# Two graph layers in fp32: ones multiplied ahead of the work, one pool per pair of x's operands, PSUM read first at the ends of phases, and row blocks spread within a step

## The chip, the core and the metric

The kernel runs on one core of one Trainium2 chip. The metric is the device time of one execution in microseconds (us), of which the median of several runs is given. Lower is better. PE is the matrix engine (TensorE), PEld its weight loads, DVE the VectorE, ACT the ScalarE, POOL the GpSimd engine and SP the SyncE, which only issues transfers here. A name with a q (SPq) is that engine's sequencer.

## The reference

x is 4096 x 512, adj is 4096 x 4096, sparse in its values but treated as dense, W is 512 x 512. All are fp32. Unused parts are left out.

```python
def _layernorm(x, axis=-1, eps=1e-5): ...

def layer0(cur, incidence_m):
    head = (incidence_m > 0).astype(incidence_m.dtype)
    head = head / jnp.maximum(jnp.sqrt(jnp.sum(head * head, axis=-1, keepdims=True)), EPS)
    inc = incidence_m + head
    return (inc @ cur) / jnp.sum(inc, axis=-1, keepdims=True)

def layer1(X, A, W):
    A2 = A + jnp.eye(A.shape[0], dtype=A.dtype)
    dscale = jnp.diagonal(A2) ** (-0.5)
    temp = A2 @ X @ W.T
    A_norm = dscale[:, None] * A2 * dscale[None, :]
    return jax.nn.relu(A_norm @ temp)

x = _layernorm(x + layer0(x, adj), axis=-1)
x = _layernorm(x + layer1(x, adj, W), axis=-1)
```

So there are three large products: inc times x, A2 times the first layer's result, and A_norm times the projected result.

## The kernel before

**Fewer products.** The big products are done by a Strassen-like scheme (the Winograd form): a 2 x 2 block product takes seven block products, with sums of the left operand (S1 to S4, made by `add_up`, L163) and of the right operand (T1 to T4). Each of the seven has a PSUM bank of its own (`bank(0)` to `bank(6)`); `bank(7)`, also called `spare()`, serves counts, projections and transposes.

**Layer 0 (n up to 63, L450 and L437).** x's operands lie in eight tiles `feats`, one for two row blocks each, all from one pool `feats_pool` (L273). `build` and `build_last` make the T sums in them. The adjacency comes in chunks of four times 128 x 512 by SP. For row block 0 (`multiply_plain`, L439) there is no scheme: it runs 2 halves x 4 chunks x 4 row steps with plain products. The positive entries of its rows are counted by `count_half` (L318): ACT makes signs, PE multiplies them by a bf16 tile of ones, `scale_half` makes the scale from the counts, and `upper_inc` or `to_inc` adds the scaled mask. For the later blocks the counts come from rows loaded as they lie (`load_natural`, a prefetch of five tiles); `count` sums signs on ACT, and `spread` (L355) makes the scale in three parts: reduce and square root, reciprocal and a diagonal tile `d`, and a product of `d` with the fp32 ones (L373). `raw_sums` also writes sums of the adjacency out to memory for layer 1, by POOL. From block 1 on `multiply1` (L423) does seven products for each of 16 row steps, and `combine` (L461) reads the seven banks.

**Layer 1 (L823 to L881).** Both products of layer 1 (k=2 and k=3) use the scheme twice, nested: 7 outer products (`p`, in the order of `ORDER`), for two column slabs `s`, each with 8 steps `kk`. In a step `multiply2` (L250) does the seven inner products of 512 columns. Its left tiles come from `tr` (loaded by `load_b`, L235) and `ts` (made from it by `sum_b`), its right tiles from `a` (loaded by `load`) and `s` (made by `prepare`, two steps ahead). After the last step of a phase `outer` (L660) takes the banks: `inner` (L639) has four outputs, made by four of its operations, which a function `put` receives; for k=2 the results of p=6 go straight to c12 and three more operations follow for each of the four (`then`, L682).

**The order around the change.** The program is in manual order: each engine executes its instructions as the Python code issues them, and pools take the place of pools that were closed. At the end of layer 0 `scope.close()` (L623) frees the operands of x, and `tops` (the pool of `tr` and `ts`), `ringx`, `workx`, `accs` and `resident` are opened in their place. In each step of layer 1 the order is: loads on SP, `prepare`, `sum_b`, what `later` holds, `multiply2`, and then one finished row block from `queue`, or two in the last phase:

```python
        while later:
            later.pop(0)()
        multiply2(n, acc)
        ...
        end = n >= len(steps) - NQ
        if 1 <= kk <= (6 if end else 5):
            for _ in range(2 if end else 1):
                if queue:
                    kind, args = queue.pop(0)
                    fetch(kind, *args)
                    kind(*args)
```

A row block is a projection (`project`, k=2) or a row block of the output (`layer1`, or `layer1_first` for half columns of two blocks). The latter transposes on PE (L746) into the spare bank, and ACT rectifies from there (L750). What remains of it (`rest`: the sum, statistics, square root, normalisation, the store; for a projection the sums and their write) is held in `later` and runs in the next step. After the last step `finish` (L797) completes the last eight row blocks.

Of the kernel before, what the change touches and what calls it, by code (L numbers as in the profile page):

```python
# [8 lines left out]
F32 = mybir.dt.float32  # L9
# [4 lines left out]
P = 128  # L14
# [12 lines left out]
def tile_adj_resnorm_d2(  # L27
# [67 lines left out]
    def spare():  # L95
        return bank(7)
# [150 lines left out]
        nc.vector.tensor_add(t[:, :, 3, :], b[:, :, 2, :], t[:, :, 2, :])  # L247
        sums_b[g] = t

    def multiply2(n, acc):  # L250
        k, s, p, kk = steps[n]
        a, sm = ready.pop(n)
        b, t = (y[n // 2][:, kk % 2] for y in (raw_b, sums_b))
        for m, (right, left) in enumerate((
            (a[:, A11, :], b[:, 0, :]), (a[:, A12, :], b[:, 2, :]), (sm[:, S2, :], t[:, 2, :]),
            (sm[:, S1, :], t[:, 0, :]), (sm[:, S3, :], t[:, 1, :]), (sm[:, S4, :], b[:, 3, :]),
            (a[:, A22, :], t[:, 3, :]),
        )):
            nc.tensor.matmul(acc[m], left, right, start=(kk == 0), stop=(kk == NQ - 1))  # L259

    def load_up_to(n):
# [4 lines left out]
    def load_b_up_to(g):  # L266
        while made["load_b"] <= min(g, len(groups) - 1):
            load_b(made["load_b"])
            made["load_b"] += 1


    scope = ExitStack()
    feats_pool = scope.enter_context(tc.tile_pool(name="feats", bufs=1))  # L273
    w1_pool = scope.enter_context(tc.tile_pool(name="w1", bufs=2))
    pools["turn"], pools["work"] = [ring] * 2, work

# [21 lines left out]
    def build(g):  # L298

        s = feats[g][:, :, :, 0:H]  # L300
        nc.vector.tensor_sub(s[:, :, T1:T3 + 1:2, :], s[:, :, B11:B22 + 1:2, :],
                             s[:, :, T4:T4 + 1, :].to_broadcast([P, 2, 2, H]))
        nc.vector.scalar_tensor_tensor(s[:, :, T2, :], s[:, :, T1, :], -1.0, s[:, :, B22, :], op0=ALU.mult, op1=ALU.subtract)

    def build_last(g):

        s = feats[g][:, :, :, 0:H]
        nc.vector.tensor_add(s[:, :, T4, :], s[:, :, B21, :], s[:, :, T2, :])
# [9 lines left out]
    def count_half(h, c, ps):  # L318

        m = w1_pool.tile([P, 2, CW], F32, name="sr", bufs=2).bitcast(BF16)[:, :, 0:CW]  # L320
        signs(m, chunks[c][:, 2 * h:2 * h + 2, :])
        for z in range(2):
            nc.tensor.matmul(ps, ones_b, m[:, z, :], start=(c + z == 0), stop=(c == NC - 1 and z == 1))

    def scale_half(h, ps):
        n = scale[0][:, h, :]
# [75 lines left out]
    def to_inc(n, h):  # L402

        y, z = masks(n, h, slice(0, CW))
        nc.vector.tensor_add(z, z, y)  # L405
# [30 lines left out]
            )):  # L436
                nc.tensor.matmul(acc[m][:, 0:w], left, b[:, right, 0:w], start=(kk == 0), stop=(kk == NP - 1))  # L437

    def multiply_plain(h, c, acc, then=None):  # L439

        a = chunks[c]
        for i in range(CK):
            kk = c * CK + i
            cols = slice(i * P, (i + 1) * P)
            if then is not None and i == 1:
                then()
            k1, k2 = (a[:, A21, cols], a[:, A22, cols]) if h else (inc11[:, c, cols], a[:, A12, cols])
            for left, ops in ((k1, (B11, T4)), (k2, (B21, B22))):
                for y, op, w in zip(acc, ops, (W, H)):
                    nc.tensor.matmul(y[:, 0:w], left, slots[kk][:, op, 0:w], start=(kk == 0 and left is k1),  # L450
                                     stop=(kk == NP - 1 and left is k2))
# [55 lines left out]
        nc.gpsimd.dma_start(out=in_outer(2, j, slice(T1, T4 + 1)), in_=t)  # L507


    feats = [feats_pool.tile([P, 2, 7, W], F32, name=f"b{g}") for g in range(NP // 2)]  # L510
    for kk in range(NP):
        slots[kk] = feats[kk // 2][:, kk % 2]
    for n in range(NC):
# [9 lines left out]
    for c in range(NC):  # L523
        load_half(0, c)
    ps = spare()
    for c in range(NC):
        count_half(0, c, ps)
    for kk in range(10):
        load_x(kk)
    for c in range(NC):  # L530
# [18 lines left out]
    build(2)  # L549
    upper_inc(3, slice(0, CW))  # L550
    ps = spare()
    multiply_plain(0, 2, top, lambda: [count_half(1, c, ps) for c in range(NC)])
    build(3)
    scale_half(1, ps)
    count(16)
    build(4)
    raw_sums(0)
    to_inc(0, 1)
    multiply_plain(0, 3, top)
    top = take(0, top)  # L560
    build(5)
# [1 line left out]
    to_inc(1, 1)  # L563
    multiply_plain(1, 0, low)
    load_chunk(NC)
    spread(1, 0)
    build(6)
    build_last(0)
    raw_sums(2)
    to_inc(2, 1)  # L570
    spread(1, 1)
    build_last(1)
    multiply_plain(1, 1, low)
    load_chunk(NC + 1)
    spread(1, 2)
# [84 lines left out]
    def outer(k, p, acc):  # L660

        (c11, c12), (c21, c22) = C_of[k]

        def into(dst, then=None):
            def put(i, op):
                op(dst[:, i, :])
                if then is not None:
                    then(i)
            inner(acc, put)

        def by_way(then):
            def put(i, op):
                y = row_tile("y", 2)
                op(y)
                then(i, y)
            inner(acc, put)

        if k == 2:
            if p in (4, 5, 1):
                into({4: c21, 5: c22, 1: c11}[p])  # L680
            elif p == 6:
                def then(i):  # L682
                    add(c12[:, i, :], c11[:, i, :])
                    nc.vector.tensor_sub(c21[:, i, :], c21[:, i, :], c12[:, i, :])
                    add(c12[:, i, :], c22[:, i, :])
                into(c12, then)
            elif p == 7:
                def then(i, y):
                    nc.vector.tensor_sub(c21[:, i, :], c21[:, i, :], y)
                    less(c22[:, i, :], y, c12[:, i, :])  # L690
                by_way(then)
            else:
                dst = {2: c11, 3: c12}[p]
                by_way(lambda i, y: add(dst[:, i, :], y))
        else:
            if p in (2, 3):
                into({2: c11, 3: c12}[p])
            elif p == 5:
                into(c22, lambda i: add(c12[:, i, :], c22[:, i, :]))
            elif p == 1:  # L700
                into(c21, lambda i: add(c11[:, i, :], c21[:, i, :]))
            elif p == 6:
                def then(i, y):
                    add(c21[:, i, :], y)
                    add(c12[:, i, :], c21[:, i, :])
                by_way(then)
            elif p == 7:
                def then(i, y):
                    add(c21[:, i, :], y)
                    less(c22[:, i, :], c22[:, i, :], c21[:, i, :])  # L710
                by_way(then)
            else:
                by_way(lambda i, y: nc.vector.tensor_sub(c21[:, i, :], y, c21[:, i, :]))
# [83 lines left out]
    def finish(h, items):  # L797

        stats = {}
        for t in range(len(items) + 2):  # L800
# [16 lines left out]
            if t > 1:  # L817
# [2 lines left out]
                normalise(o, *stats[b])  # L820
                nc.sync.dma_start(out=out[b * P:(b + 1) * P, :], in_=o)

    load_b_up_to(0)  # L823
    load_up_to(2)
    load_b_up_to(2)
# [4 lines left out]
    for n, (k, s, p, kk) in enumerate(steps):  # L830
        if kk == 0:
            acc = [bank(m) for m in range(7)]
        load_up_to(n + LA + PF)
        if n + LA < len(steps):
            prepare(n + LA)
        if n % 2 == 0 and n // 2 + 1 < len(groups):
            sum_b(n // 2 + 1)
        while later:
            later.pop(0)()
        multiply2(n, acc)  # L840
        if n == 0:
            layer0(NP - 1, C)
        elif n == 1:
            operands(NP - 1, C)
            nc.gpsimd.dma_start(out=wt, in_=w_t.rearrange("(a p) o -> p a o", p=P))
        if n % 2 == 1:
            load_b_up_to(n // 2 + 3)
        end = n >= len(steps) - NQ
        if 1 <= kk <= (6 if end else 5):
            for _ in range(2 if end else 1):  # L850
                if queue:
                    kind, args = queue.pop(0)
                    fetch(kind, *args)
                    kind(*args)
            for kind, args in queue[:2]:
                fetch(kind, *args)
        if kk == NQ - 1:
            outer(k, p, acc)
            if (k, p) in DONE:
                h = DONE[k, p]  # L860
                items = blocks(h, s)
                if n + 1 < len(steps):
                    queue.extend(((project, layer1)[k - 2], (h, b)) for b in items)
            if n == len(steps) - 1 - NQ:
                items = sorted(blocks(1, s), key=lambda b: b[1])
                queue.extend((layer1_first, (1, *items[i:i + 2])) for i in range(0, len(items), 2))
            for kind, args in queue[:2]:
                fetch(kind, *args)
        if n + 1 == len(steps) // 2:

            scope.close()
            ring3 = ctx.enter_context(tc.tile_pool(name="ring3", bufs=2))
            late["pool"] = ctx.enter_context(tc.tile_pool(name="late", bufs=1))
            i = made["a"] % 4
            pools["turn"] = [ring3] * 2 + pools["turn"][i:] + pools["turn"][:i]
            made["a"] = 0
            PF = 3
    while later:
        later.pop(0)()
    assert not queue  # L880
    finish(1, items)  # L881


# [30 lines left out]
```

## Time and profile before

| | us |
|---|---|
| median of 3 runs | 2327.46 (2325.59 to 2328.12) |
| the profiled execution, own time | 2326.3 |
| its span in the profile | 2324.4 |
| PE busy | 2278.8 (98%) |
| PE weight loads busy | 1355.4 (58%) |
| DVE busy | 1817.9 (78%) |
| ACT busy | 353.7 (15%) |
| POOL busy | 220.3 (9%) |
| chain that ended last | PE 93%, DVE 4%, DMA 2%, issue 1% |

All times in the views are counted from the start of the span. A row of a timeline has the start, the length, the engine, the line of the code, the operation, output and inputs by the program's names, their sizes and the count; in brackets stands the idle time of the engine before it, and what ended that. In the chain of waits a row has the start, the length, the engine (or DMA) and the line. An fp32 product of the code is two matmul instructions on PE. The granted clock is the share of the full PE clock.

### The profile page before, as it was taken

To read this page: it belongs to the slowest core of one execution; us is meant where nothing else is said; L and a number is where in the kernel's file an instruction comes from. 1 tells how busy PE (TensorE), PEld (TensorE's weight loads), DVE (VectorE), ACT (ScalarE), POOL (GpSimd) and SP (SyncE) were. 2 spreads that over 40 slices of the span, in tenths; PEclk is the share of its full clock that TensorE was granted. 3 is DMA by queue.
4 is the path that set the end of the run, shared out by engine and by line. 5 is a ranking of instruction groups with operands and counts; after the bars stand their busy time and mean duration, and the time that the engine had idled before them with its cause. 6 is when DMAs were issued, how large, how long until landed. Compare 5 with 4: busy or idle time off the path is not lost.

```text
span 2324.4 us, 21026 instructions
## 1 busy us (share of the span) xinstructions
PE 2278.8 (98%) x7182; PEld 1355.4 (58%) x7182; DVE 1817.9 (78%) x2631; ACT 353.7 (15%) x815; POOL 220.3 (9%) x357
## 2 busy tenths in 40 slices
PE   7999999999999999999999999999999999999996
PEld 6888888888888834444444444444444444444443
DVE  5998988989988777787666778776567798767796
ACT  4323322333222000000000000000000011200013
POOL 0111111111111100000111000011100000000010
PEclk9999999999999999999999999999999999999998
DMA  9777777777776466575566746477665576765572
GB/s 319 253 263 252 251 265 257 243 255 265 262 247 223 167 261 263 199 261 201 205 254 252 275 180 253 160 276 266 231 236 215 219 256 241 262 238 212 219 262 77
DMA packets 148443, 551.93 MB, mean 237 GB/s; under 512 B 15968, under 2 KB 24176, under 8 KB 109936
## 3 DMA queue, kind: packets, MB, share of 16 engines
q1 hardware_dynamic: 114624, 417.38, 51.2%
q0 software_dynamic: 33712, 133.21, 15.6%
q8 instruction: 57, 0.93, 0.2%
q14 instruction: 50, 0.41, 0.0%
HBM read 437.27 MB, written 113.25 MB: 237 GB/s over the span
## 4 chain that ended last, share of the span: by engine, by line
PE 93%; DVE 4%; DMA 2%; issue 1%; ACT 0%; SPq 0%; ACTq 0%; DVEq 0%
PE q L259 54%; PE q L437 31%; PE q L726 5%; PE q L450 2%; DMA a<-oa 1%; DVE s L166 1%; PE q L746 1%; DMA a<-adj_r 0%; DVE c L654 0%; DMA s<-adj_q 0%; DVE s L168 0%; PE q L373 0%; DMA a<-adj_q 0%; DVE c L658 0%; DVE r L232 0%
## 5 line engine op out<-in xcount | busy, mean ns | idle before, releaser
L259 PE MATMUL q<-s,ts 128*128 128x512 f32 x1344 | 614.5, 593 | 2.0 <-DVE u L645 1.9
L437 PE MATMUL q<-b,s 128*128 128x256 f32 (+1 forms) x1920 | 454.4, 379 | 0.2 <-DVE s L168 0.2
L166 DVE TENSOR_TENSOR s<-a 128x1024 f32<-128x1024 f32 x236 | 288.8, 1224 | 207.5 <-PE q L259 169.5
L259 PEld LDWEIGHTS q<-s,ts 128*128 128x128 f32 x1344 | 256.0, 191 | 325.5 <-issue 295.7
L437 PEld LDWEIGHTS q<-b,s 128*128 128x128 f32 x1920 | 363.8, 190 | 52.6 <-DVE s L168 0.6
L437 PE MATMUL q<-b,a 128*128 128x258 f32 (+1 forms) x1440 | 354.0, 380 | 0.0
L259 PE MATMUL q<-a,tr 128*128 128x512 f32 x704 | 334.8, 598 | 5.3 <-DMA tr<-ob 4.3
L437 PEld LDWEIGHTS q<-b,a 128*128 128x128 f32 x1440 | 273.3, 190 | 38.5
L259 PE MATMUL q<-s,tr 128*128 128x512 f32 x448 | 228.9, 593 | 0.0
L259 PEld LDWEIGHTS q<-a,tr 128*128 128x128 f32 x704 | 132.8, 192 | 163.4 <-issue 157.8
L312 ACT ACTIVATE nat<-nat,tiny 128x512 f32<-128x512 f32 x240 | 171.0, 715 | 181.4 <-DMA nat<-adj 180.6
L259 PE MATMUL q<-a,ts 128*128 128x512 f32 x352 | 180.3, 594 | 3.3 <-DVE c L650 2.9
L168 DVE TENSOR_TENSOR s<-a,s 128x512 f32<-128x512 f32 x236 | 163.3, 692 | 8.1
L169 DVE TENSOR_TENSOR s<-a,s 128x512 f32<-128x512 f32 x236 | 163.3, 692 | 8.0
L398 DVE SCALAR_TENSOR_TENSOR mask<-a,sc 128x1024 f32<-128x1024 f32 (+2 forms) x129 | 154.2, 1197 | 2.1
L405 DVE TENSOR_TENSOR a<-a,mask 128x1024 f32<-128x1024 f32 x123 | 150.7, 1225 | 6.6 <-DVE mask L398 0.5
L259 PEld LDWEIGHTS q<-s,tr 128*128 128x128 f32 x448 | 85.3, 190 | 107.0 <-issue 100.8
L643 ACT COPY p<-q 128x512 f32<-128x512 f32 x28 | 16.4, 585 | 756.0 <-PE q L259 756.0
L259 PEld LDWEIGHTS q<-a,ts 128*128 128x128 f32 x352 | 66.7, 190 | 88.7 <-issue 76.4
L726 PE MATMUL q<-wt,c 128*128 128x512 f32 x256 | 115.1, 593 | 0.0
L166 DVE TENSOR_TENSOR s<-r 128x1024 f32<-128x1024 f32 x48 | 58.7, 1224 | 68.7 <-PE q L259 62.4
L388 POOL DMA_DIRECT2D oa<-sr x64 | 57.7, 901 | 390.2 <-DVE sr L381 250.8
(134 smaller groups left out, 1695.0 us busy)
## 6 DMA issues: line engine op xcount, KB each, us to landing
a<-adj_r SPq DMA_DIRECT2D x112, 1024.0 KB, 6.1
a<-oa SPq DMA_DIRECT2D x80, 1024.0 KB, 5.3
nat<-adj SPq DMA_DIRECT2D x240, 256.0 KB, 7.2
a<-adj_q SPq DMA_DIRECT2D x60, 1024.0 KB, 6.0
tr<-ob SPq DMA_DIRECT2D x112, 512.0 KB, 3.7
oa<-sr POOLq DMA_DIRECT2D x64, 512.0 KB, 7.9
oa<-r POOLq DMA_DIRECT2D x32, 1024.0 KB, 6.7
y<-x POOLq DMA_DIRECT2D x64, 256.0 KB, 7.2
```

The costliest lines, as they stand in the source:

```text
L166: nc.vector.tensor_add(s[:, S3:S1 + 1, :], a[:, A11:A22 + 1, :], a[:, A21, :].unsqueeze(1).to_broadcast([P, 2, w]))
L168: nc.vector.tensor_add(s[:, S2, :], a[:, A11, :], s[:, S1, :])
L169: nc.vector.tensor_add(s[:, S4, :], a[:, A12, :], s[:, S2, :])
L259: nc.tensor.matmul(acc[m], left, right, start=(kk == 0), stop=(kk == NQ - 1))
L312: nc.scalar.activation(y, a, AF.Sign, bias=tiny, scale=2.0 ** 64, accum_out=accum)
L388: nc.gpsimd.dma_start(out=dst, in_=sr.rearrange("p m (k i) -> p (m k) i", i=P))
L398: nc.vector.scalar_tensor_tensor(m, v, 0.0, s.unsqueeze(1).to_broadcast(list(v.shape)), op0=ALU.is_gt, op1=ALU.mult)
L405: nc.vector.tensor_add(z, z, y)
L437: nc.tensor.matmul(acc[m][:, 0:w], left, b[:, right, 0:w], start=(kk == 0), stop=(kk == NP - 1))
L450: nc.tensor.matmul(y[:, 0:w], left, slots[kk][:, op, 0:w], start=(kk == 0 and left is k1), stop=(kk == NP - 1 and left is k2))
L726: nc.tensor.matmul(pv, C_of[2][h][f][:, 2 * r + e, cols], wt[:, 2 * f + e, :], start=(f + e == 0), stop=(f + e == 2))
L746: nc.tensor.transpose(ps[:, at + i * P:at + (i + 1) * P], C_of[3][h][d // 2][:, 2 * r + d % 2, cols], ident)
```

## The change

It has five parts.

1. `idle_products` multiplies the fp32 tile of ones by itself into a bank that is not in use: 8 times before the first counts, 3 times after each of the first three counts and 11 times after the fourth.
2. Each of the eight tiles of x's operands has a pool of its own.
3. In `multiply_plain(0, 2, ...)` the second counts are taken two by two, ahead of row steps 0 and 2, not all four ahead of step 1. `build(4)` goes behind `to_inc(0, 1)`; `spread(1, 0)` goes behind `to_inc(2, 1)`, and `build_last(1)` ahead of `spread(1, 1)`.
4. `into` lets `inner` make all four outputs before it runs `then` for the four.
5. In each step of layer 1 the row blocks are taken out of the queue ahead of `multiply2`. Of two, the first is done inside `multiply2`, ahead of its fourth product, the second after it. The rests of the step before run after the new row blocks, not ahead of `multiply2`.

```diff
-    def multiply2(n, acc):
+    def multiply2(n, acc, between=None):
...
+            if m == 3 and between is not None:
+                between()
             nc.tensor.matmul(acc[m], left, right, start=(kk == 0), stop=(kk == NQ - 1))
...
-    feats_pool = scope.enter_context(tc.tile_pool(name="feats", bufs=1))
+    feats_pools = [scope.enter_context(tc.tile_pool(name=f"feats{g}", bufs=1)) for g in range(NP // 2)]
...
+    def idle_products(times):
+        for _ in range(times):
+            nc.tensor.matmul(bank(2)[:, 0:P], ones_f, ones_f, start=True, stop=True)
...
-    def multiply_plain(h, c, acc, then=None):
+    def multiply_plain(h, c, acc, then={}):
...
-            if then is not None and i == 1:
-                then()
+            if i in then:
+                then[i]()
...
-    feats = [feats_pool.tile([P, 2, 7, W], F32, name=f"b{g}") for g in range(NP // 2)]
+    feats = [pool.tile([P, 2, 7, W], F32, name=f"b{g}") for g, pool in enumerate(feats_pools)]
...
     ps = spare()
+    idle_products(8)
     for c in range(NC):
         count_half(0, c, ps)
+        idle_products(3 if c < NC - 1 else 11)
...
-    multiply_plain(0, 2, top, lambda: [count_half(1, c, ps) for c in range(NC)])
+    multiply_plain(0, 2, top, {i: lambda i=i: [count_half(1, c, ps) for c in (i, i + 1)] for i in (0, 2)})
     build(3)
     scale_half(1, ps)
     count(16)
-    build(4)
     raw_sums(0)
     to_inc(0, 1)
+    build(4)
...
     load_chunk(NC)
-    spread(1, 0)
     build(6)
     build_last(0)
     raw_sums(2)
     to_inc(2, 1)
+    spread(1, 0)
+    build_last(1)
     spread(1, 1)
-    build_last(1)
     multiply_plain(1, 1, low)
...
         def into(dst, then=None):
-            def put(i, op):
-                op(dst[:, i, :])
-                if then is not None:
+            inner(acc, lambda i, op: op(dst[:, i, :]))
+            if then is not None:
+                for i in range(4):
                     then(i)
-            inner(acc, put)
...
+    def take_up(item):
+        kind, args = item
+        fetch(kind, *args)
+        kind(*args)
...
-        while later:
-            later.pop(0)()
-        multiply2(n, acc)
+        end = n >= len(steps) - NQ
+        items = [queue.pop(0) for _ in range(min(len(queue), 2 if end else 1))] if 1 <= kk <= (6 if end else 5) else []
+        held = later[:]
+        later.clear()
+        multiply2(n, acc, (lambda: take_up(items.pop(0))) if len(items) > 1 else None)
...
-        end = n >= len(steps) - NQ
+        for item in items:
+            take_up(item)
+        for rest in held:
+            rest()
         if 1 <= kk <= (6 if end else 5):
-            for _ in range(2 if end else 1):
-                if queue:
-                    kind, args = queue.pop(0)
-                    fetch(kind, *args)
-                    kind(*args)
             for kind, args in queue[:2]:
                 fetch(kind, *args)
...
-    finish(1, items)
+    finish(1, blocks(1, s))
```

The list that `finish` gets is the same one, under another name.

## The prediction

> **What bounds the kernel now.** I read the profile from the coarse to the fine. First the stretches by stage, since a mean over the span hides where an engine stops. Columns: stretch, length, busy time (and instructions) of PE, PEld, DVE, ACT, POOL, granted clock, DMA share, GB/s.
>
> ```profile
> core 0: us, PE busy (x) PEld busy (x) DVE busy (x) ACT busy (x) POOL busy (x), PEclk, DMA share, GB/s
> 0.00:80.00 80.00, 65.64 (x277) 53.13 (x278) 54.05 (x69) 28.26 (x60) 8.01 (x35) 1.00 0.95 317
> 80.00:813.00 733.00, 732.82 (x3384) 641.32 (x3383) 647.20 (x919) 211.78 (x561) 116.97 (x164) 1.00 0.73 245
> 813.00:860.00 47.00, 41.60 (x92) 17.79 (x91) 31.04 (x58) 2.21 (x5) 3.87 (x6) 0.93 0.70 267
> 860.00:2255.00 1395.00, 1389.84 (x3298) 619.20 (x3297) 1037.68 (x1476) 90.83 (x149) 86.61 (x143) 1.00 0.64 235
> 2255.00:2305.00 50.00, 44.77 (x121) 21.05 (x120) 33.99 (x66) 9.79 (x19) 4.81 (x9) 0.97 0.26 95
> 2305.00:2324.40 19.40, 4.15 (x17) 2.92 (x15) 13.90 (x47) 10.84 (x24) 0.00 (x0) 0.59 0.29 108
> ```
>
> PE is the bound: 2123 of 2128 us in the two long stretches. The change leaves their products alone, so it can only win in the 80 us in front, the 47 at the layer change, the 50 at the end, and 5.2 us of holes between. What makes each hole is in the chain that ended last (start, length, what):
>
> ```profile
> 750.30 63.70 PE q L437 x294
> 814.06 4.07 DMA tr<-ob
> 818.26 2.04 PE q L259 x2
> ...
> 1012.04 1.24 DVE s L166
> ...
> 1021.25 0.70 DVE c L684
> 1023.32 30.35 PE q L259 x70
> ```
>
> At 814.06 the last product of layer 0 ends and only then is `tr` loaded. At 1012 to 1023 the chain lies on DVE. Then the timelines: PE in front and at the end (start, length, count, idle before and releaser), and DVE at two places.
>
> ```profile
> 17.56 1.92 PE L450 MATMUL q<-b,a 128*128 128x258 f32 x4
> 22.95 1.03 PE L450 MATMUL q<-b,a 128*128 128x258 f32 x4
> ```
>
> ```profile
> 2266.44 0.60 PE L746 MATMUL q<-ident,c 128*128 128x128 f32 x4
> 2270.52 0.89 PE L746 MATMUL q<-ident,c 128*128 128x128 f32 x4 [3.48 <-ACT o L750]
> 2271.20 3.38 PE L259 MATMUL q<-a,tr 128*128 128x512 f32 x4
> ```
>
> ```profile
> 57.93 0.17 DVE L359 TENSOR_REDUCE n<-cnt 128x2 f32<-128x16 f32 x1 [6.54 <-ACT nat L312]
> ```
>
> ```profile
> 1014.64 0.68 DVE L644 TENSOR_TENSOR c<-q,p 128x512 f32<-128x512 f32 x1
> ...
> 1031.45 0.42 DVE L246 SCALAR_TENSOR_TENSOR ts<-ts,tr 128x256 f32<-128x256 f32 x1
> ```
>
> L450 starts one instruction per 0.43 us until 21.4, and per 0.216 after: half clock at first. (The clock column shows 1.00 there only because no record precedes 21.4.) The same after the two long idles: 818.3 to 823.5 and 2270.8 to 2274.2 have clock 0.50.
>
> **Front (ones, counts, spread).** An fp32 product is two PE instructions. No row has a 128-column fp32 product, so I bound it: below by the 128-column transposes (0.212 us per instruction at half clock, 0.109 at full), above by the 256-column L450 (0.43, 0.216). I take the transposes, since L450 to L259 show time going with columns. Eight products then take 3.4 us from 2.6, when `ones_f` is set, and end at 6.0, before the first counts (6.39); three between counts take 1.3 us slow, 0.65 fast. With PE some 90% busy from 2.6 on, I put the clock up at about 8. The last count still waits for its signs (11.23) and ends near 11.7 instead of 12.29, so the first L450 moves from 15.71 to 15.1; eleven products (2.4 us) fill most of that wait.
> From there PE needs 16 row steps at 8 x 0.216 = 1.73: 27.7 us, plus 1.7 for the second counts. Those lost 3.35 us at 34.2 to 37.6, as the third signs waited for the first count's buffer (two `sr`). Now ACT has two steps, 3.5 us, for its 2.3 us of signs, whose data landed by about 30. So layer 0's first half ends at 44.5 instead of 49.7: 5.2 earlier (0.6 start, 2.8 clock, 1.7 counts). The DVE keeps up: `to_inc(0,1)` ends near 40.8 and `to_inc(1,1)` near 48.2, for use at 44.5 and 51.5.
> What is late next: `spread(1,0)` needs 16 row counts, paced by their loads, until 57.9. Before, DVE stood there 6.5 us with `build(6)`, `build_last(0)`, `raw_sums(2)`, `to_inc(2,1)` (6.0 us) queued behind it; now they come first. `d` is then ready at 59.75 instead of 64.9, while PE arrives at 58.4: PE waits 1.35 us (before 1.4). DVE's work from 57.9 to the first S2 of block 1 shrinks from 22.8 to about 17 us, S2 at about 75.2 instead of 80.7. Front gain 5.4. Against it: three `raw_sums` writes now fall into the counting instead of two. DMA share there is 0.93 to 0.96. The Trainium skill (DMA: Bandwidth & Descriptors, Issuing engines are not separate DMA queues) says that transfers of all issuers share the same 16 engines and interleave; by it 0.5 MB at 310 GB/s costs up to 1.7 us, by the trace's five-deep prefetch perhaps nothing. I take 0.8: **front 4.6** (2 to 6.5).
> A second rule: TensorE: Matmul & The Clock Gate, Part 1, asks about 3.4 us of sustained work in a free-running window for full clock. The trace has dense work from 15.71 and full clock only at 21.42. If the broken pattern of ones is not enough, PE is 2.8 us later at the spread, of which 1.35 was waiting: 1.5 lost. By the rule alone 0.
>
> **Pools apart.** One pool held all of x's operands, so `tr` waited for the last reader at 814.06. The eight pools are 14.4 KB per partition each; `tr`, `ts` and the extra `a` lie over the first two, last read in the block's first chunk, before 778. SP reaches `tr` right after the load at 801.9; nothing on SP stands in front. DVE is idle from 804.2, so `sum_b(0)` is done early and `combine` follows PE's last products, ending at about 815 instead of 822.7. PE goes on at 814.0: the second step starts at 820.0 instead of 827.16, **7.1** (4.3 wait, 2.8 half clock, which goes since there is no idle). Late next: step 5's `a`, behind `tr` of group 3 on SP, which waits for the POOL writes of the last rows. Before: PE lost 1.4 at 850.8. That chain moves with `combine`, 20.3 us after its end, so `tr` issues at 835.3 and PE needs step 5 at 844.1, 0.6 us more room than before; fewer transfers are bunched behind it. I take **0.5** (-0.3 to 1.4).
>
> **PSUM first.** Only `into` with a `then` changes, and only k=2, p=6 had holes: 3.0 us at 1016 to 1023, 2.5 at 1411 to 1418. With seven reads in 4.9 us PE does not wait in the next step. But the twelve other operations (8.3 us) still run before the next `prepare` and `sum_b`. DVE has no gap from 1012.04 to 1031.9, and in the next phase's third step PE took the S2 product at 1032.01, 0.1 us after `ts` was ready (1031.45 and 0.42). So the wait goes to that product, two steps on. All that remains is the tighter order on DVE (0.61 instead of 0.72 us between independent operations), about 0.4 each: **0.8** (0 to 5.5).
>
> **Row blocks spaced.** In the last phase two blocks per step shared one PSUM bank back to back; rectify (0.69) lay between, and at 2266.9 it also queued on ACT behind the square roots and normalisations of the step before. Now one comes after three products (2.57 us), one after the other four (3.43), and the held rests come behind both rectifies on ACT. From 2252.50: step 2 at 2259.38 (was 2260.43), step 3 at 2266.27 (2271.20), step 4 at 2273.15 (2280.74), step 5 at 2279.6 (2287.18). Closest is the second transpose of step 3 at 2272.7, whose bank is free at 2271.9. `prepare` for step 5 ends near 2273.3: no DVE bound. **7.6** (4 to 8): 5.4 waits, 1.5 half clock, 0.7 small. Of the tail from 2305 nothing changes.
> Holding the rests also moves them elsewhere. On POOL, a projection's write of `t` is queued behind the next block's writes: it lands about 5.6 us into the next step, where DVE wants `t` at 2.6 to 4.1; done by 7.9 of a 9.44 us step. In layer 1, the square root waits on ACT for the next rectify, so DVE stands until 7.5 us into the step and starts the next `prepare` about 1.4 late; `prepare` is two steps (12.9 us) ahead of its use. Both at nothing; without that cover 1.4 per step.
>
> **Sum.** 4.6 + 7.1 + 0.5 + 0.8 + 7.6 = 20.6. The profiled execution took 2326.3 (span 2324.4): 2305.7. The median of the runs lies 1.2 above it: 2306.9, say 2307.
>
> **Rivals.** (1) The pools do not come free apart: `tr` still at 814.06. For it: nothing but that the trace has no case of split pools; against: `tr` waited for the last reader of all, as one pool would. Loses 7.6: 2314.5. (2) The PSUM order wins its full 5.5, if DVE finds slack I do not see: 2302. Against: the gapless DVE run. (3) The front gives 1 to 2 only, its counts later by their DMAs or the clock still half: 2310. (4) Slower: the held square roots. Place: about 20 single blocks of layer 1; DVE stands 1.4 us in each. Should that lateness reach PE, 20 x 1.4 = 28 us is lost and the time is 2335. It decides once DVE is over 11 us late at a `prepare`; I find 1.4, not growing, because a late DVE waits less.
>
> **How the numbers follow.** A measurement of this kernel can tell about 0.2%, 4.7 us. The sum as worked out 0.68, within 4 us; (1) 0.09; (2) 0.07; (3) 0.09; (4) 0.05; nothing gained in all 0.02. Faster 0.93, same 0.02, slower 0.05. The range 2300 to 2312.5 takes in the first, (2) and (3).
>
> **What would show it.** L450 at 0.216 us from its first instruction; no wait of ACT signs for PE near 35; the spread still waiting about 1.3 us, for DVE. `tr` issued near 802 less the front's gain, clock 1.00 throughout the layer change. At p=6 no hole in the next phase's first step, but one of about 2.6 us at its third step's S2, waiting for `ts`. No wait for ACT at L746 before the tail. The prediction is wrong if `tr` still waits for L437, if PE stops in single-block steps, or if the holes at p=6 go without a later one.

## Result and profile after

The changed kernel takes 2314.41 us (median of 11 runs, 2311.66 to 2323.46); the kernel before took 2328.12 in its 11 runs beside it (2325.59 to 2330.42). The ratio is 0.9952, 95% interval 0.9939 to 0.9965: faster, by 13.7 us where 20.5 were forecast, and 1.9 us above the range that was given (2300 to 2312.5). The profiled execution took 2313.43 us, its span is 2311.4, 13.0 shorter than before.

First the same stretches by stage, of the kernel after (length, busy time and instructions of PE, PEld, DVE, ACT and POOL, granted clock, DMA share, GB/s). The fifth stretch is cut at 2295, as its end moved.

```profile
0.00:80.00 80.00, 75.99 (x320) 60.95 (x322) 53.92 (x68) 27.29 (x57) 8.01 (x35) 1.00 0.91 306
...
813.00:860.00 47.00, 46.48 (x116) 21.48 (x115) 36.07 (x66) 2.80 (x6) 3.87 (x6) 1.00 0.77 291
860.00:2255.00 1395.00, 1389.71 (x3304) 618.42 (x3303) 1030.78 (x1474) 90.64 (x151) 86.56 (x143) 1.00 0.64 234
2255.00:2295.00 40.00, 37.85 (x105) 17.48 (x103) 33.35 (x65) 8.90 (x18) 4.81 (x9) 1.00 0.26 93
```

In the layer change PE now has 46.48 of 47 us busy, at clock 1.00, where it had 41.60 at 0.93; the end is at 1.00 too. The first row misleads: PE has 10 us more busy time in the front, and none of it is work that the result needs. The long stretch still lacks 5.3 us of PE, as it did before.

The chain that ended last, after (start, length, what), at the four places where it was shown of before, and at the front:

```profile
8.59 0.80 PE q L331 x2
...
24.18 0.49 PE q L331 x2
24.67 5.42 PE q L458 x25
...
752.48 63.68 PE q L445 x294
816.16 21.99 PE q L261 x52
838.15 8.46 DMA a<-adj_r
...
1024.91 21.74 PE q L261 x50
```

At 816.16 the chain goes from PE to PE: the transfer of `tr` is gone from it. The transfer at 838.15 is that of step 5's `a`, which stood in the chain before as well. But layer 0's last product ends at 816.16 instead of 814.06, so the front has lost 2.1 us instead of gaining 4.6. The front's chain says why: it is made of L331, the products on ones, that were to lie in PE's idle time. The timeline of PE in front, first two rows of before, then after (start, length, count, in brackets idle time before and releaser):

```profile
6.39 1.01 PE L323 MATMUL q<-sr,ones_b 128*128 128x512 bf16 x2 [6.39 <-ACT sr L312]
...
15.71 2.05 PE L450 MATMUL q<-b,s 128*128 128x258 f32 x4 [3.43 <-issue]
```

```profile
2.61 6.77 PE L331 MATMUL q<-ones_f 128*128 128x128 f32 x16 [2.61 <-POOL b L545]
9.17 1.06 PE L326 MATMUL q<-sr,ones_b 128*128 128x512 bf16 x2
10.03 2.34 PE L331 MATMUL q<-ones_f 128*128 128x128 f32 x6
12.16 1.06 PE L326 MATMUL q<-sr,ones_b 128*128 128x512 bf16 x2
...
18.13 0.85 PE L326 MATMUL q<-sr,ones_b 128*128 128x512 bf16 x2
18.82 5.85 PE L331 MATMUL q<-ones_f 128*128 128x128 f32 x22
24.50 1.03 PE L458 MATMUL q<-b,s 128*128 128x258 f32 x4
```

PE's row after shows no idle time, and yet sixteen instructions take 6.77 us. One product (two instructions) follows another after 0.85 us at half clock, and after 0.55 at full. The counts (L326) start at 9.17, 12.16, 15.15 and 18.13; before, they started at 6.39, 7.59, 10.00 and 11.27. The first row product (L458) starts at 24.50, before at 15.71. Lengths tell the clock: six L331 take 2.34 us up to 18.3, and 22 take 5.85 after; the record of the granted clock goes to full at 18.63. What hides in the gapless PE row is in the row of the weight loads:

```profile
2.61 0.50 PEld L331 LDWEIGHTS q<-ones_f 128*128 128x128 f32 x2 [2.61 <-POOL b L545]
3.46 0.50 PEld L331 LDWEIGHTS q<-ones_f 128*128 128x128 f32 x2 [0.35 <-PE q L331]
```

Each product waits 0.35 us with its weights for the product before it, an output of PE itself. `idle_products` takes `bank(2)` anew for each product, as a new tile, and the new tile waits for the last writer of the old one (shown below, by the run with one bank).

The signs on ACT are made to wait too, since their two buffers are read by the counts (timeline of ACT, after):

```profile
10.32 1.15 ACT L315 ACTIVATE sr<-a,tiny 128x1024 bf16<-128x1024 f32 x1 [2.81 <-PE q L326]
```

At p=6, the timeline of PE and two rows of DVE's, after:

```profile
1024.91 1.55 PE L261 MATMUL q<-s,ts 128*128 128x512 f32 x3 [1.69 <-DVE ts L246]
```

```profile
1020.52 0.69 DVE L664 TENSOR_TENSOR c<-c,c 128x512 f32<-128x512 f32 x1
...
1024.43 0.42 DVE L246 SCALAR_TENSOR_TENSOR ts<-ts,tr 128x256 f32<-128x256 f32 x1
```

The hole has gone from the next phase's first step to its third, and waits for `ts`, which DVE makes when the twelve operations are done. At the end, PE's timeline after has its transposes (L755) between products, with no bracket:

```profile
2259.59 1.02 PE L261 MATMUL q<-a,ts 128*128 128x512 f32 x2
2260.45 0.60 PE L755 MATMUL q<-ident,c 128*128 128x128 f32 x4
2260.89 1.88 PE L261 MATMUL q<-a,tr 128*128 128x512 f32 x4
```

And there are waits that the prediction did not have (PE's timeline, after):

```profile
1897.65 2.84 PE L261 MATMUL q<-s,ts 128*128 128x512 f32 x6 [0.33 <-DVE u L655]
...
1902.09 1.12 PE L261 MATMUL q<-a,ts 128*128 128x512 f32 x2 [0.74 <-DVE y L660]
```

From start to start, less the usual pace, these cost 0.50 and 0.90 us, and one like them near 2245 costs 0.47.

### The profile page after: what moved, and what is told of

Same layout as the page of the kernel before. It is cut to its first block, busy times and chain, and to the rows that moved or that the text cites. A ratio compares the mean times of both kernels' runs of the same rounds, so it can differ in the third digit from the quotient of the medians.

```text
span 2311.4 us, 21136 instructions
## 1 busy us (share of the span) xinstructions
PE 2286.4 (99%) x7237; PEld 1361.8 (59%) x7238; DVE 1813.0 (78%) x2631; ACT 351.5 (15%) x815; POOL 220.2 (10%) x357
## 3 DMA queue, kind: packets, MB, share of 16 engines
q0 software_dynamic: 33712, 133.21, 15.7%
## 4 chain that ended last, share of the span: by engine, by line
PE 93%; DVE 5%; DMA 1%; issue 0%; ACT 0%; POOL 0%; ACTq 0%; DVEq 0%; SPq 0%; POOLq 0%
PE q L261 53%; PE q L445 31%; PE q L735 5%; PE q L458 2%; PE q L331 1%; DMA a<-adj_r 1%; DVE s L166 1%; DVE c L664 1%; PE q L755 1%; DMA a<-oa 0%; DVE s L168 0%; DVE r L224 0%; PE q L381 0%; DVE c L693 0%; PE q L326 0%
```

## Experiments

Each kernel was timed beside the kernel before (medians 2328.18, 2327.74 and 2327.76 us in the three sets). Letters in the expectations: A, that the products on ones are the loss; D, that the held rests make PE wait at the ends of phases; E, that a bank taken anew makes each product wait for the one before; G, that the `then` operations can be put where DVE has time. Other letters are the rivals set against them. In the diffs, - is the kernel named in the text.

**Without the ones.** The kernel after, less its products on ones.

```diff
-    idle_products(8)
...
-        idle_products(3 if c < NC - 1 else 11)
```

> The changed kernel without its products on ones. Theory A (the ones hold up the first counts): the last count ends near 12.3 us instead of 18.8, the first row product starts at 15.7 instead of 24.5, at half clock until about 21, and block 1 starts near 76.3 instead of 82.2: about 2308, 6 less than the changed kernel, and less scatter between runs. Rival B (the front is late through the new places of the second counts and of spread, or through the earlier writes of raw_sums): block 1 stays near 82, the time at 2314.

Measured: 2311.31 us (2310.43 to 2314.59, 5 runs), ratio 0.9932 [0.992, 0.9944]. PE's timeline in front and at block 1, of this kernel:

```profile
11.06 1.01 PE L326 MATMUL q<-sr,ones_b 128*128 128x512 bf16 x2 [0.27 <-ACT sr L315]
15.49 2.05 PE L458 MATMUL q<-b,s 128*128 128x258 f32 x4 [3.43 <-issue]
17.34 1.92 PE L458 MATMUL q<-b,a 128*128 128x258 f32 x4
...
20.28 1.03 PE L458 MATMUL q<-b,a 128*128 128x258 f32 x4
...
75.33 1.03 PE L445 MATMUL q<-b,a 128*128 128x258 f32 x4
```

It runs at half clock until 19.8 (1.92 us for four, 1.03 later) and still reaches block 1 at 75.33, where after reaches it at 82.16. So the ones are the loss (A), and not the new places of the counts and of the spread (B). By the medians the gain is 3.1 us, where 6 were expected. The profile shows where the rest went: at p=6 PE loses 2.59 and 2.11 us instead of 1.85 and 2.14, 1.7 more in a stretch of half clock behind the second hole, 1.2 more at step 5, and about 1 at the ends of two other phases.

**Ones alone.** The kernel before with `idle_products` and its calls as in the change.

> The kernel before with the products on ones alone. Theory A: the last count ends near 18.8, the first row product starts at 24.5, block 1 near 84 instead of 80.5: about 2331, 3 slower than before. Rival B (the ones are harmless): faster by up to 3, about 2325.

Measured: 2331.69 us (2328.06 to 2339.07, 12 runs), ratio 1.002 [1.0009, 1.0031]: slower, as expected. In its profile the clock is full at 12.8, so the first row product starts at 22.08, not at 24.5, and block 1 at 81.36, not at 84 (before: 79.5).

**Ones with more columns.** To see whether the narrow products were the trouble, the kernel after with one bf16 product over a whole bank for each fp32 one.

```diff
+    ones_w = w1_pool.tile([P, CW], BF16, name="ones_w", bufs=1)
+    nc.gpsimd.memset(ones_w, 1.0)
...
-            nc.tensor.matmul(bank(2)[:, 0:P], ones_f, ones_f, start=True, stop=True)
+            nc.tensor.matmul(bank(2), ones_b, ones_w, start=True, stop=True)
```

> As many products on ones, but each is one bf16 instruction of 512 columns in place of an fp32 product of 128 columns (two instructions). This is the length that the prediction had counted with: 0.43 us at half clock, 0.22 at full. Theory A: eight end near 6.0, full clock by 9.4 at the latest, since PE now streams without holes, the last count ends near 11.7, the first row product starts near 15.1 at full clock, block 1 near 75.3: about 2307. Rival C (ones never wake the clock, whatever their width): half clock until about 21, block 1 near 78: about 2310.

Measured: 2314.39 us (2312.1 to 2317.4, 5 runs), ratio 0.9942 [0.993, 0.9954]; block 1 at 76.60. A miss of some 7 us in the time. The row of weight loads shows what was overlooked:

```profile
4.22 0.10 PEld L333 LDWEIGHTS <-ones_b 128*128 128x128 bf16 x1 [0.54 <-issue]
```

They come 0.64 us apart (0.54 idle and 0.10 busy), though two instructions of the counts, of 512 columns too, follow each other in 0.43 at half clock (in the profile after the next work starts at 10.03, two instructions behind 9.17). A gap between products is left whatever their width, so it is not the columns. The front is 5.6 us better than after's all the same (76.60 against 82.16). This profile, of the slowest of the five runs (2317.4), gave that back at p=6: 3.07 us in each hole, with 3.4 us of half clock, a loss of 1.7, after each.

**One bank, taken once.** The kernel after with all products on ones writing the same tile.

```diff
+    ones_q = bank(2)
     idle_products(8)
...
-            nc.tensor.matmul(bank(2)[:, 0:P], ones_f, ones_f, start=True, stop=True)
+            nc.tensor.matmul(ones_q[:, 0:P], ones_f, ones_f, start=True, stop=True)
```

> The changed kernel, but all its products on ones write to one tile of bank 2, taken once, where each took the bank anew. Theory E (what makes them dear is not their width: each product waits until the one before has left the bank, which shows as the weight load's idle time 0.35 us, released by PE): the waits go, eight products take about 3.4 us instead of 6.6 and end before the first signs are ready, full clock near 10, the last count ends near 11.7, block 1 starts near 75.3: about 2308, without the runs of over 2317. Rival F (the fp32 weight loads, 0.29 to 0.33 us at half clock, set the pace): still 0.43 per instruction, 2314.

Measured: 2308.16 us (2306.88 to 2311.23, 5 runs), ratio 0.9923 [0.991, 0.9935]. PE's timeline of this kernel:

```profile
2.62 3.54 PE L331 MATMUL q<-ones_f 128*128 128x128 f32 x16 [2.62 <-POOL b L546]
...
11.62 2.62 PE L331 MATMUL q<-ones_f 128*128 128x128 f32 x22
15.21 1.10 PE L458 MATMUL q<-b,s 128*128 128x258 f32 x4 [0.97 <-issue]
...
59.94 0.67 PE L381 MATMUL q<-d,ones_f 128*128 128x256 f32 x2 [1.06 <-DVE d L376]
...
76.26 2.00 PE L445 MATMUL q<-b,s 128*128 128x256 f32 x8 [0.91 <-DVE s L168]
```

Nothing but the tile is changed, and the same sixteen instructions take 3.54 us instead of 6.77. The clock is full at 5.76, the counts start where the signs let them, and the S2 of block 1 starts at 76.26 (before: 80.74). All five runs are below the fastest of the changed kernel (2311.66), whose 11 runs reach up to 2323.46. That is the wait shown (E), and the weight loads do not set the pace (F): an instruction takes 0.22 us with the same loads.

**Rests ahead of the products again.** The kernel after, with the held rests run ahead of `multiply2` except in the last phase.

```diff
         held = later[:]
         later.clear()
+        if not end:
+            for rest in held:
+                rest()
+            held = []
```

> The changed kernel, but outside the last phase the held rests run ahead of multiply2 again. Theory D (a square root behind the next rectify on ACT makes DVE late, and the lateness reaches the ends of the phases): the waits of PE at 1897, 1901 and 2245 us (0.5, 0.9, 0.5) go, about 2312.5. Rival: they come from PE now being earlier against DVE, and stay; 2314.4.

Measured: 2317.5 us (2314.01 to 2321.93, 5 runs), ratio 0.9957 [0.9945, 0.997]. PE's timeline of this kernel at the end of the phase that had the new waits, and in front:

```profile
1899.95 1.02 PE L261 MATMUL q<-s,tr 128*128 128x512 f32 x2
1900.81 1.02 PE L261 MATMUL q<-a,ts 128*128 128x512 f32 x2
```

```profile
18.99 9.17 PE L331 MATMUL q<-ones_f 128*128 128x128 f32 x22
27.95 1.92 PE L458 MATMUL q<-b,s 128*128 128x258 f32 x4
```

The three waits are gone, so the held rests made them (D). The time is no lower: 2312.5 was expected. In this profile the clock came up only at 30.7, with block 1 at 86.98. The ones are the same code here as in after and in the run of ones alone; the clock came up at 30.7, 18.6 and 12.8. As an experiment on time it decides nothing. It was repeated on top of the one bank, where the clock does not stand in the way:

> The same, and outside the last phase the held rests run ahead of multiply2 again. Theories E and D add up: 2308 less 1.9, about 2306, with no waits near 1897 and 2245. If D's gain was lost to something else, 2308.

Measured: 2307.19 us (2303.94 to 2309.02, 4 runs), ratio 0.9913 [0.99, 0.9927]; no waits near 1897 and 2245. Its median is 1.0 below that of one bank alone, less than the runs scatter; the gain of 1.9 is seen in the profile only. The profiles have another source of scatter, at the ends of the phases near 1056 and 1452: PE is idle there for 2.6 us in all in this run and 1.7 in the one with one bank alone, 0.2 in after. In this run DVE had stood 1.40 us just before, at 1049, for a transfer of `a`.

**The twelve operations later.** On top of the last kernel, `then` goes into `later`, to run behind the next step's `prepare` and `sum_b`.

```diff
-                for i in range(4):
-                    then(i)
+                later.extend(lambda i=i: then(i) for i in range(4))
```

> The same as the one with one bank and the rests back, and the twelve operations after PSUM was read are put into `later`, so that DVE does the next step's prepare and sum_b before them. Theory G (the hole at p=6 is DVE's backlog of 8.3 us ahead of prepare, which the change only moved): the waits of PE for ts near 1020 and 1415 (1.9 to 3.1 us each, and half clock after them in some runs) go: about 2301. Rival H (the backlog then hits the step after it, one step later): as without it, 2306.

Measured: **2301.08 us** (2299.62 to 2303.18, 4 runs), ratio 0.9891 [0.9876, 0.9906]. DVE at the end of p=6, and the PE waits of this kernel (total, times, longest):

```profile
1005.92 0.68 DVE L662 SCALAR_TENSOR_TENSOR c<-u,p 128x512 f32<-128x512 f32 x1
1006.52 1.22 DVE L166 TENSOR_TENSOR s<-a 128x1024 f32<-128x1024 f32 x1
...
1009.83 0.42 DVE L246 SCALAR_TENSOR_TENSOR ts<-ts,tr 128x256 f32<-128x256 f32 x1
1010.63 0.68 DVE L665 TENSOR_TENSOR c<-c,c 128x512 f32<-128x512 f32 x1
```

```profile
PE q L755 <- DVE c L722: 3.2, 3, 1.3
...
PE q L261 <- DMA a<-adj_r: 1.0, 1, 1.0
...
PE q L261 <- DVE y L661: 0.5, 1, 0.5
...
```

`ts` does not stand in the list any more, left-out rows included: it comes before the twelve operations, which run while PE multiplies, and no wait comes a step later (H). All four runs are below the fastest of the kernel named last (2303.94). This is the fastest version, 13 us under the changed kernel by the medians.

**What the ones are worth when done well.** The last kernel without them:

> The same, without any products on ones. By theories A and E the ones are worth only the half clock from 15.5 to 21 (2 to 3 us), of which some is hidden behind the counts that spread waits for: equal to the one with ones within 2 us, 2301 to 2303. If a broken pattern of ones hurts even without the bank waits, faster than that one by over 2.

Measured: 2302.78 us (2302.63 to 2304.35, 4 runs), ratio 0.9897 [0.9884, 0.9911]; half clock from 15.4 to 21.6, block 1 at 76.18 where the fastest version has it at 73.23. The intervals overlap, so a worth of the ones is not shown: 1.7 us by the medians, 3 at block 1 in these two profiles. With one bank alone it was nothing at block 1's S2 (76.26, against 76.20 without ones): the waits for the spread (1.06) and for S2 (0.91) took what the ones had gained. `ts` stands in no row of this kernel's waits either, and it is some 8 us faster than the first one without ones (2311.31), which shows the last two edits together a second time.

**Parts alone.** The kernel before with one part of the change each. Pools apart:

> The kernel before with one edit: a pool of its own for each of the eight tiles of x's operands. All theories: no wait for the last product at the layer change, tr issued near 802, clock 1.00 there. By the forecast's sum 7.1 for the wait and the half clock and 0.5 for step 5: 2320.5 beside the kernel before. If a part of that gain was owed to another edit (the front's, which moves the whole layer), it is under 6: over 2322.

Measured: 2321.32 us (2316.9 to 2323.89, 8 runs), ratio 0.9969 [0.9959, 0.998]. No wait for `tr`, no half clock there; step 5 loses 1.26 and 0.24 us, as much as before (1.4). So the 7.1 at the layer change holds by itself (6.4 by the medians of the whole time); the further 0.5 does not show.

PSUM read first:

> The kernel before with one edit: at the end of a phase all four outputs are read from PSUM ahead of the twelve operations that follow. Theory that DVE's work only moves: the hole at p=6 (3.0 and 2.5 us) turns into one of about 2 us at the third step of the next phase, waiting for ts: gain 0.8 to 1.5, 2326.5 to 2327.5, the same within what can be told. Rival, that the wait itself was the loss: gain 5.5, 2322.5, with no hole later.

Measured: 2327.54 us (2322.97 to 2331.46, 13 runs), ratio 0.9999 [0.999, 1.0007]: no difference. PE's timeline of this kernel has the hole two steps on:

```profile
1030.66 1.55 PE L259 MATMUL q<-s,ts 128*128 128x512 f32 x3 [2.50 <-DVE ts L246]
```

Row blocks spaced and rests held:

> The kernel before with one edit: row blocks taken up inside the step and rests held behind them. Theory that the held square roots cost as well as gain: the waits for ACT at the transposes of the last phase go (7.5), three new waits of 0.5, 0.9 and 0.5 us come at the ends of the p=7 phase of the last product (1.9): net 5.6, 2322.5. Rival, that these new waits came from another part of the change: 7.5, 2320.5, with no wait near 1901, 1905 and 2252.

Measured: 2323.11 us (2320.71 to 2324.16, 11 runs), ratio 0.9979 [0.9971, 0.9988]. The waits at the transposes are gone and the three new waits (0.50, 0.90, 0.47 us) are there, without any other part of the change. The net is 4.7 by the medians, beside 5.6 expected.

The order of counts, `build` and spread:

> The kernel before with one edit: second counts two by two, build(4) and the spread later; no products on ones. Theory: 1.7 for the lost wait at the counts, 1.4 for the spread that PE no longer waits for, and a part of the 1.3 of S2: block 1 at 75.5 to 76.5, 3 to 4 us gained: 2324 to 2325. That is nearly all that the front gained in the run without products on ones (block 1 at 75.33). Rival, that the three raw_sums writes in the counting delay the loads: block 1 at 78 or later, gain under 2.

Measured: 2323.41 us (2320.68 to 2326.3, 21 runs), ratio 0.9985 [0.9979, 0.9992]; the second counts and the spread wait for nothing, and block 1 starts at 76.17, so a delay by the three writes of `raw_sums` does not show. By the medians 4.4, a little over the 3 to 4 expected.

By the medians the four parts give 6.4, 0.2, 4.7 and 4.4, together 15.7; all four at once, in the kernel without ones, gave 16.9 (2328.18 less 2311.31). With the ones the change gives 13.7. So the ones take about 3 of what the other parts earn. The sum of the parts and the whole agree within what the medians can tell.

## Why the prediction was wrong in size

The direction and most of the mechanisms were right; one term of the sum came out with the other sign, and another was set to nothing. The measured 2314.41 is nearly the number of rival (1), 2314.5, but by chance: that rival had `tr` still waiting for layer 0, which it does not.

| term | forecast | measured in the profile after |
|---|---|---|
| front | 4.6 | -2.1 (814.06 to 816.16) |
| pools apart | 7.1 | 7.1 |
| step 5 | 0.5 | 0.6, not seen with the pools alone |
| PSUM first | 0.8 | 1.5, not seen with it alone |
| row blocks | 7.6 | 7.5 |
| rests held | 0 | -1.9 |
| sum | 20.6 | 12.7; the span moved 13.0 |

**Front: the step that failed** is "I take the transposes". The price taken was 0.424 us per product, with an end at 6.0; measured were 0.85 and 9.2. The transposes' pace itself was right, as the one-bank kernel shows: 3.54 us for sixteen, forecast 3.4. What was missed is the wait between products. It could be read in the diff: `bank(2)` stands inside the loop, so each product takes the bank anew. The upper bound of 0.86 was the right number by chance; its reason, more columns, was not at work. From this the rest of the term failed: the clock was not up at 8 but at 18.6, the counts started 3 to 7 us later than before, and eleven further products, meant to fill a wait of 3.4 us, took 5.7 us and held up the first row product until 24.50. With the wait taken away and nothing else, the working holds: last count at about 11.6 (forecast 11.7), first row product at 15.21 (15.1), spread wait 1.06 (1.35), S2 at 76.26 (75.2, or 76.0 with the 0.8 set aside for transfers), and the time 2308.16, where 2307 was forecast, though the 1.9 of the held rests are still in it.

The second rule weighed there, about 3.4 us of sustained work (TensorE: Matmul & The Clock Gate, Part 1, of the Trainium skill), was put at a loss of at most 1.5. The runs bear it out: with ones back to back the clock was full 3.1, 5.7 and 5.7 us after the first of them (the three kernels with one bank and ones), and in the profiles without ones 3.1 to 6.2 us after the first row product. With a gap in each product it took 10.2, 16.0 and 28.1 us of the same code. The price of a broken pattern was not 1.5, since the ones themselves run in PE's order ahead of the counts, and at half clock they last longer. Rival (3), a front that gains little with the clock still half, was the right kind of case; it was priced at 1 to 2 us of gain, and left no room for a loss.

**Held rests, "both at nothing".** The lateness of DVE was seen (1.4 us) and its cover, a `prepare` two steps ahead, was named; within the steps the cover held, and rival (4) with 28 us did not come. It was not asked of the one place where PE waits for DVE at once: the end of a phase, where the seven banks must be read before the next step can write them. There the lateness came out as 0.5, 0.9 and 0.47 us.

**What was right.** `tr` is issued at 804.5 (about 802 plus the 2.1 lost in front), the clock is 1.00 through the layer change, and 7.1 is what it gives. At p=6 the hole went to the third step's S2, waiting for `ts`: 1.85 and 2.14 us against about 2.6. In the last phase the waits for ACT and the half clock behind them are gone: 7.5 against 7.6. PE waits for no signs any more: its list of waits has no entry of ACT's. That PE does not wait for the spread either was not forecast (about 1.3): the late front gives DVE the time. The 1.5 of half clock within the 7.6 were there before in the profile that was read, but not in every profile of that code: with the pools alone the same wait, 3.47 us, has no half clock behind it (the last section says why).

## What to carry to other kernels

Work put into an idle engine lies in its order, and delays what is behind it if it runs over: price it with the waits that its own buffers make, by looking in the diff for a buffer that is taken anew in each pass. An engine row with no idle time is not proof of full pace; compare the time per instruction with a known one, and read the row of the weight loads. When a wait is removed by moving work, ask where the same work stands next: here the twelve operations paid only when they went behind what PE needed. And a stretch of half clock behind a hole can stand in one profile of a code and not in the next, so compare several before it is priced into a forecast.

## What the runs showed of the hardware

The clock comes back at a time that the code does not fix: 12.8, 18.6 and 30.7 us in three profiles of the same products with gaps, 5.8 to 8.3 in three profiles without gaps. The same part of the Trainium skill says that the window runs freely, so that the number of slow products varies from run to run; these traces agree. In all fourteen of them, the 52 times between two changes of the granted clock are whole multiples of 3.413 us, on a grid that lies differently in each run. At half clock a product took 0.42 us with one bank and 0.85 with the gap, so with the gap half of a window stays empty (an estimate from these two); it seems to need a window with enough of the counts, or of the row products, to bring the clock up.

A hole of 2 to 3 us in a long run at full clock can also bring the clock down. After holes at p=6, four kernels show 3.4 us at half clock, for instance the one without ones (its PE timeline):

```profile
1415.21 4.54 PE L261 MATMUL q<-s,ts 128*128 128x512 f32 x6 [1.94 <-DVE ts L246]
```

Six instructions take 4.54 us there, and 2.84 behind the same hole in after. The length of the hole does not decide it, but where it lies on the grid. The run with wide ones and the run with one bank both have a hole of 3.07 us there. These are the grid's windows around it, first with wide ones, then with one bank (columns as in the stretches by stage):

```profile
1018.47:1021.88 3.41, 0.66 (x2) 0.00 (x0) 3.31 (x5) 0.00 (x0) 0.00 (x0) 1.00 1.01 413
1021.88:1025.29 3.41, 3.25 (x4) 1.52 (x5) 3.31 (x6) 0.00 (x0) 0.00 (x0) 0.50 0.01 2
```

```profile
1016.11:1019.52 3.41, 1.90 (x5) 0.57 (x3) 3.31 (x5) 0.00 (x0) 0.00 (x0) 1.00 0.87 296
1019.52:1022.93 3.41, 2.02 (x5) 1.06 (x6) 3.31 (x6) 0.00 (x0) 0.00 (x0) 1.00 0.41 166
```

In the first the hole falls almost whole into one window, PE is busy for 0.66 us of it, and the next window has clock 0.50. In the second the end of a window cuts the hole in two, and the clock stays at 1.00. Over all fourteen traces this has no exception: in the 33 windows after which the clock fell from full to half, PE was busy for 1.55 us or less by its records, and in every window after which it stayed full, for 1.59 or more. So a hole that falls into one window can cost about 1.7 us (half of 3.41) more than its length, from about 1.9 us on (an estimate: 3.41 less 1.55); the same hole on the seam of two windows costs its length alone.
